# A pre-norm transformer block in fp32: from the seventh batch on, projections read the raw input transposed by the host, and the norm is applied to their products

## The chip, the cores and the metric

The kernel runs on one core of a Trainium2 chip. The metric is device time in microseconds of one execution, as a median over several runs. The profile was taken of one further execution; a clock share of 1.000 means that TensorE was never throttled in it.

TensorE multiplies matrices (PE in the profile; PEld are its weight loads), VectorE (DVE) and ScalarE (ACT) work element by element, GpSimd (POOL) does masks and small things, and SyncE (SP) issues DMA transfers. Each engine executes its own instructions in order. PSUM is the memory that TensorE writes to.

## What is computed

One layer over 16 batches of 256 tokens with 256 channels, all in fp32. Cut from the reference:

```python
def _layernorm(x, axis=-1, eps=1e-05):
    m = jnp.mean(x, axis=axis, keepdims=True)
    v = jnp.var(x, axis=axis, keepdims=True)
    return (x - m) / jnp.sqrt(v + eps)

def attn(x, wq, wk, wv, wo):                # 16 heads of 16, S = 256
    q, k, v = x @ wq.T, x @ wk.T, x @ wv.T  # split into heads
    scores = einsum('bihd,bjhd->bhij', q, k) * HEAD_DIM ** -0.5
    scores = where(j - i > 16, -inf, scores)
    return einsum('bhij,bjhd->bihd', softmax(scores), v) @ wo.T

def ffn(h, gate_w, up_w, down_w):           # 256 -> 1024 -> 256
    return (silu(h @ gate_w.T) * (h @ up_w.T)) @ down_w.T

x = x + attn(_layernorm(x), wq, wk, wv, wo)
x = x + ffn(_layernorm(x), gate_w, up_w, down_w)
```

The three feed-forward weights are not given but interpolated from control points (Catmull-Rom splines).

## The kernel before

Everything is written out in order. Five wrappers, one for each engine, keep every instruction in program order (line 88 is the wrapper, so nearly every instruction has L88 in the profile). What the profile calls `x8` for `pq` are four matmuls: an fp32 matmul leaves two records there, an fp32 transpose one.

The outer loop (line 647) runs 20 steps `s`. In step `s` three batches are in work at once: the maxima of the scores of batch `nb = s - 1`, the exponentials and value products of batch `tb = s - 2`, and the division, output projection, second norm and feed-forward of `ob = s - 3` and of the one before it. A step alternates `inner` and `outer` blocks of scores (four inner, two outer) with other work in seven gaps; `project(s, gap)` and `fill(s, gap)` say what goes into a gap. The scores of `nb` and of `tb` share two PSUM tiles. VectorE reads the maxima from them (`z`, `mx`), ScalarE the exponentials (`e`). A block of scores can only start when both have been through with the block before.

Around the change these stages matter:

- `stats_a`, `norm_a` (lines 225 to 229): mean and variance of a batch's tokens on VectorE, the power -1/2 on GpSimd (`rstda`), then `xna = (x - mean) * rstd` on VectorE, with two instructions.
- `turn_a` (231): four transposes on TensorE (`pta`) into PSUM, one copy on ScalarE into `xnT`.
- `project_qk` (235): four matmuls for q (`pq`) and four for k (`pk`) from `xnT`; ScalarE copies them to `qkc`, q times 1/4. `spread` (252): eight DMA transfers bring `qkc` to the layout of the scores (`qk`). `project_v` (262): four matmuls (`pv`), two ScalarE copies into `v`.
- `turn_max` (387): maxima transposed (`pm`), copied (`mxT`) and sent by four small transfers into `qk`, where the next step's scores of that batch subtract them.
- `gather`, `invert`, `divide`, `project_o` (417 to 467): the value products `au` are moved to `ac`, the softmax sums to `den`; their reciprocals go out to DRAM (`rd`) and come back broadcast (`rb`); `ac` is multiplied by them, projected (`py`) and added to `x`. `stats_f`, `norm_f`, `turn_f` make the second norm's `xnf`, `ptf`, `x2T`; `gate_up` (`pg`, `pu`) and `down` (`pd`) are the feed-forward.

From step 4 on `project` is regular: with `pb = s + 2`, statistics of `pb + 1` in gap 1, norm of `pb + 1` and projection and spread of `pb` in gap 2, the turn of `pb + 1` in gap 4, v of `pb` in gap 6. In steps 0 to 3 the dictionary `projections` says which stage goes where; the dictionary `heads` says in which gaps the spline weights are made (`spline`, tiles `pw`) and how many idle matmuls (`keep_running`, tile `run`) are put in.

PSUM has two buffers each for the pools `ps_f` (tag f: `pg`, `pu`, `pd`, `run`, half of `pw`) and `ps_m` (tag m: `pq`, `pk`, `pv`, `po`, `pta`, `py`, `ptf`, `pm`, the other half of `pw`). All transfers but the first few are issued by SyncE, in program order; a transfer that has to wait holds up what is issued after it. Each transfer also waits until the eighth before it has landed.

In the first microseconds ScalarE's queue loads the four attention weights; SyncE's loads `x` of batches 0 and 1, the spline table `tab`, control points `cp_in` (three parts), `x` of batch 2, the selection mask `second`, and `x` of batch 3.

Of the kernel before, what the change touches and what calls it, by code (L numbers as in the profile page):

```python
# [18 lines left out]
P = 128  # L19
# [74 lines left out]
def block_kernel(  # L94
    ctx: ExitStack,
    tc: tile.TileContext,
    x: bass.AP,
    wqT: bass.AP,
    wkT: bass.AP,
    wvT: bass.AP,  # L100
# [11 lines left out]
    const = ctx.enter_context(tc.tile_pool(name="const", bufs=1))  # L112
    sb = ctx.enter_context(tc.tile_pool(name="sb", bufs=2))
    sb1 = ctx.enter_context(tc.tile_pool(name="sb1", bufs=1))
    sb4 = ctx.enter_context(tc.tile_pool(name="sb4", bufs=4))
    sb6 = ctx.enter_context(tc.tile_pool(name="sb6", bufs=6))
    sbx = ctx.enter_context(tc.tile_pool(name="sbx", bufs=10))
# [5 lines left out]

    xs = {}

    def load_x(b, engine):
        xs[b] = sbx.tile([P, 2, DIM], F32, tag="x", name=f"x{b}")
        engine.dma_start(xs[b], x[b].rearrange("(c p) d -> p c d", p=P))

    AHEAD = 2  # L130
    load_x(0, sp)
    w_in = {}
    for nm, src in (("q", wqT), ("k", wkT), ("v", wvT), ("o", woT)):
        t = const.tile([P, 2, DIM], F32, tag=f"w{nm}", name=f"w{nm}")
        act.dma_start(t, src.rearrange("(kc p) o -> p kc o", p=P))
        w_in[nm] = t
    load_x(1, sp)
    tab_in = const.tile([P, NPART + 2 * P], F32, tag="tab", name="tab_in")
    sp.dma_start(tab_in, tab)
    cp_in = const.tile([P, 3, NPART], F32, tag="cp", name="cp_in")  # L140
    second_in = const.tile([P, 2, NROW], mybir.dt.uint8, tag="second", name="second_in")
    for w in range(3):
        sp.dma_start(cp_in[:, w, :], cps[w])
        if w == 0:
            load_x(2, sp)
            sp.dma_start(second_in, second)
    load_x(3, sp)


    ident = const.tile([P, P], F32, tag="ident", name="ident")  # L150
    make_identity(nc, ident)
    neghalf = const.tile([P, 2], F32, tag="neghalf", name="neghalf")
    pool.memset(neghalf, -0.5)
    mask0 = const.tile([P, JB], F32, tag="mask0", name="mask0")
    mask1 = const.tile([P, S], F32, tag="mask1", name="mask1")
    masks = (mask0, mask1)
# [26 lines left out]
    downT = const.tile([P, 8, DIM], F32, tag="downT", name="downT")  # L183


    xns, xnTs, mxs, aus, aos, recs, x2s, x2Ts = ({} for _ in range(8))
    es, inters, qkcs = {}, {}, {}

    moments = {}
# [1 line left out]
    def norm_stats(b, nm):  # L191
        stats = sb.tile([P, 2, 6], F32, tag=f"stats{nm}", name=f"stats{nm}{b}")
        mv = sb.tile([P, 2, 2], F32, tag=f"mv{nm}", name=f"mv{nm}{b}")
        for c in range(2):
            dve.bn_stats(stats[:, c, :], xs[b][:, c, :])
            dve.bn_aggr(mv[:, c, :], stats[:, c, :])
        rstd = sb.tile([P, 2], F32, tag=f"rstd{nm}", name=f"rstd{nm}{b}")
        dve.tensor_scalar_add(rstd, mv[:, :, 1], EPS)
        pool.tensor_tensor(rstd, rstd, neghalf, ALU.pow)
        moments[b, nm] = mv, rstd  # L200
# [24 lines left out]
    def stats_a(b):  # L225
        norm_stats(b, "a")

    def norm_a(b):
        xns[b] = normed(b, "a")

    def turn_a(b):
        xnTs[b] = sb.tile([P, 2, S], F32, tag="xnT", name=f"xnT{b}")
        transposed(xns.pop(b), xnTs[b], f"ta{b}")

    def project_qk(b):
        qkcs[b] = qkc = sb.tile([P, 2, 2, S], F32, tag="qkc", name=f"qkc{b}")
        for i, nm in enumerate("qk"):
            pq = ps_m.tile([P, 2, S], F32, tag="m", name=f"p{nm}{b}")
            for oc in range(2):
                for kc in range(2):  # L240
                    pe.matmul(
                        pq[:, oc, :],
                        lhsT=w_in[nm][:, kc, oc * P : (oc + 1) * P],
                        rhs=xnTs[b][:, kc, :],
                        start=(kc == 0),
                        stop=(kc == 1),
                    )
            act.activation(
                qkc[:, i], pq, AF.Copy, scale=HD**-0.5 if nm == "q" else 1.0
            )  # L250

    def spread(b):
        qkc = qkcs.pop(b)
# [8 lines left out]
    def project_v(b):  # L262
        pv = ps_m.tile([P, 2, DIM], F32, tag="m", name=f"pv{b}")
        for c in range(2):
            for kc in range(2):
                pe.matmul(
                    pv[:, c, :],
                    lhsT=xnTs[b][:, kc, c * P : (c + 1) * P],
                    rhs=w_in["v"][:, kc, :],
                    start=(kc == 0),  # L270
                    stop=(kc == 1),
                )
        for c in range(2):
            act.copy(
                vs[b % NQK][:, c, :, 0:HD],
                pv[:, c, :].rearrange("p (h d) -> p h d", d=HD),
            )
        del xnTs[b]

# [41 lines left out]
    def inner(nb, tb, g):  # L323
        has_n, has_t = 0 <= nb < B, 0 <= tb < B
        qn, qt = qks[nb % NQK], qks[tb % NQK]
        if has_n:
            if g == 0:
                mxs[nb] = sb.tile([P, 2, H], F32, tag="mx", name=f"mx{nb}")
            scores(qn, True, g, P, S, P + HB + LOOK)
        if has_t:  # L330
            scores(qt, False, g, HB, HB - LOOK, S - HB + LOOK)
        if has_n:
            scores(qn, True, g, P + HB, S, S)
        if has_t:
            scores(qt, False, g, 0, 0, S)
        def exponentials(pr):
            e = sb6.tile([P, 2, S], F32, tag="e0", name=f"e0{tb}_{g}_{pr}")
            act.activation(e, tiles[pr][:, :, 0:S], AF.Exp)

            pool.affine_select(  # L340
                out=e[:, :, 0:M0], in_=e[:, :, 0:M0],
                compare_op=ALU.is_ge, fill=0.0, base=LOOK,
                pattern=[[0, 2], [1, M0]], channel_multiplier=-1,
            )
            es[tb, 0, g, pr] = e

        def maxima(pr):
            for r in (2 * pr, 2 * pr + 1):
                find_max(nb, g, r, 1, S, S)

        read(exponentials if has_t else None, maxima if has_n else None)

    def outer(nb, tb, g2):
# [10 lines left out]
        def exponentials(pr):  # L364
# [4 lines left out]
                    :, :, :, W0 - W1 : W0  # L369
                ],  # L370
                AF.Exp,
            )
            pool.affine_select(
                out=e[:, :, :, 0:P], in_=e[:, :, :, 0:P],
# [181 lines left out]
    def do(stage, b, *args):  # L556
        if 0 <= b < B:
            stage(b, *args)

    heads = {
        (0, 7): (0, 6),
        (1, 1): (1, 0), (1, 4): (1, 2), (1, 5): (1, 2), (1, 6): (0, 5), (1, 7): (0, 5),
        (2, 1): (1, 0), (2, 3): (1, 6), (2, 5): (1, 1), (2, 6): (0, 4),
        (3, 3): (0, 5), (3, 6): (0, 6),
    }
    parts = iter([(w, part) for part in range(2) for w in range(2)] + [(2, 0), (2, 1)])

    def keep_running(n):
        run = ps_f.tile([P, 2 * S], F32, tag="f", name="run")
# [2 lines left out]

    def fill(s, gap):

        n, idle = heads.get((s, gap), (0, 0))
        if idle:
            keep_running(idle)  # L580
        for _ in range(n):
            spline(*next(parts))

        alone = s > B
        late = s >= B - AHEAD
        for what, at in (
# [9 lines left out]

    projections = {
        (0, 1): ((stats_a, 1),),  # L600
        (0, 2): (
            (norm_a, 1), (coefficients, 0), (coefficients, 1), (stats_a, 2),
            (scores_and_values, 1), (scores_and_values, 2), (project_qk, 0), (spread, 0),
        ),
        (0, 4): ((turn_a, 1), (norm_a, 2)),
        (0, 6): ((project_v, 0),),
        (1, 1): ((turn_a, 2), (coefficients, 2)),
        (1, 2): ((project_qk, 1), (spread, 1)),
        (1, 3): ((project_qk, 2), (spread, 2), (scores_and_values, 3)),
        (1, 6): ((project_v, 1),),  # L610
        (1, 7): ((stats_a, 3), (norm_a, 3), (project_v, 2)),
        (2, 1): ((turn_a, 3), (stats_a, 4), (scores_and_values, 4)),
        (2, 2): ((norm_a, 4), (project_qk, 3), (spread, 3)),
        (2, 4): ((turn_a, 4),),
        (2, 6): ((project_v, 3),),
        (2, 7): ((stats_a, 5), (norm_a, 5), (project_qk, 4)),
        (3, 1): ((turn_a, 5), (stats_a, 6)),
        (3, 2): ((norm_a, 6), (spread, 4), (project_qk, 5), (spread, 5)),
        (3, 3): ((project_v, 4),),
        (3, 4): ((turn_a, 6),),  # L620
        (3, 6): ((project_v, 5),),
    }

    def project(s, gap):
        if s < 4:
            todo = projections.get((s, gap), ())
        else:
            pb = s + AHEAD
            todo = {
                1: ((stats_a, pb + 1),),  # L630
                2: ((norm_a, pb + 1), (project_qk, pb), (spread, pb)),
                4: ((turn_a, pb + 1),),
                6: ((project_v, pb),),
            }.get(gap, ())
        for stage, b in todo:
            do(stage, b)


    for t in tiles:
# [7 lines left out]
    for s in range(B + 4):  # L647
# [5 lines left out]
        fill(s, 1)  # L653
        inner(nb, tb, 1)
        do(invert, ob)
        if s + 2 + AHEAD < B:
            load_x(s + 2 + AHEAD, sp)
        project(s, 2)
        fill(s, 2)
        outer(nb, tb, 0)  # L660
# [7 lines left out]
        inner(nb, tb, 3)  # L668
        do(project_o, ob)
        do(stats_f, ob)  # L670
        fill(s, 5)
        do(norm_f, ob)
        outer(nb, tb, 1)
        fill(s, 6)
        do(turn_f, ob)
        project(s, 6)
        do(turn_max, nb)
        project(s, 7)
        fill(s, 7)
# [29 lines left out]
```

## Time and profile before

| | us |
|---|---|
| median of three runs | 673.51 |
| lowest and highest of them | 672.9, 677.17 |
| the profiled execution's own time | 670.9 |
| its span, first to last instruction | 669.2 |

| engine | busy us | share of the span |
|---|---|---|
| TensorE, matmuls | 652.2 | 97% |
| VectorE | 358.5 | 54% |
| ScalarE | 230.3 | 34% |
| GpSimd | 128.1 | 19% |

The instructions concerned, from the page's groups: `pta` 64 transposes, 287 ns mean; `xnT` 16 ScalarE copies of 588 ns; `xna` 32 VectorE instructions of 453 ns; `qkc` 32 ScalarE copies of 597 ns; `v` 32 ScalarE copies of 376 ns. A mean duration is the time from an instruction's start to its end; instructions of one engine overlap, so what a row of them takes is read from their starts, or from the chain of work, which counts each moment once. SyncE's share says nothing of the engines: only the places where something waits for its transfers matter.

### The profile page before, as it was taken

Reading aid. Unit: us, or ns where it says so; the run is one execution under the profiler, and the core shown is the slowest. Engines: PE = TensorE matmul, PEld = TensorE weight load, DVE = VectorE, ACT = ScalarE, POOL = GpSimd, SP = SyncE. Lnnn points to the kernel's source line nnn. Section 1 sums busy time; section 2 is a strip of 40 time slices with the busy share of each in tenths; the row PEclk is TensorE's granted clock in tenths of the full one; section 3 lists DMA queues with packets and bytes.
Section 4 is the critical chain, followed back from the end, with each engine's and each line's share of the span. In section 5 each row is a group of like instructions: output and inputs, shape, how many; then the busy total and the mean of one; then the engine's idle time right before and its main releaser. Section 6 shows DMA issues by size and latency. Waiting matters only on the chain.

```text
span 669.2 us, 18583 instructions
## 1 busy us (share of the span) xinstructions
PE 652.2 (97%) x7484; PEld 511.6 (76%) x7484; DVE 358.5 (54%) x1473; ACT 230.3 (34%) x413; POOL 128.1 (19%) x250
## 2 busy tenths in 40 slices
PE   7999989999999999999999999999999999999998
PEld 6666767877778787777878777787877777776876
DVE  6576556556464645645464564545455565623332
ACT  2345434243342424334242433423233333333110
POOL 5222212111121211112121121211112121212000
PEclk9999999999999999999999999999999999999999
DMA  8422142113030210313031121303010101010100
GB/s 253 64 40 35 37 82 61 35 23 66 24 77 19 66 33 20 65 27 73 20 72 27 22 63 27 59 19 62 22 30 24 25 14 36 18 45 24 34 17 16
DMA packets 34422, 29.65 MB, mean 44 GB/s; under 512 B 7840, under 2 KB 33696, under 8 KB 34336
## 3 DMA queue, kind: packets, MB, share of 16 engines
q1 hardware_dynamic: 32928, 27.15, 18.1%
q10 hardware_dynamic: 1408, 1.31, 0.7%
q8 instruction: 59, 0.97, 0.6%
q14 instruction: 27, 0.22, 0.1%
HBM read 10.88 MB, written 4.46 MB: 23 GB/s over the span
## 4 chain that ended last, share of the span: by engine, by line
PE 94%; ACT 2%; DVE 2%; DMA 1%; issue 1%; POOL 0%; SPq 0%; ACTq 0%; DVEq 0%
PE pg L88 18%; PE pd L88 17%; PE pu L88 17%; PE scores L88 14%; PE po L88 6%; PE pq L88 5%; PE py L88 5%; PE pk L88 4%; PE pv L88 4%; PE pta L88 1%; PE ptf L88 1%; PE run L88 1%; PE pw L88 1%; ACT e L88 1%; DMA qk<-qkc 1%
## 5 line engine op out<-in xcount | busy, mean ns | idle before, releaser
L88 ACT ACTIVATE e<-scores 128x512 f32<-128x512 f32 (+1 forms) x192 | 117.4, 615 | 252.2 <-PE scores L88 188.5
L88 DVE CUSTOM_DVE_ANT_0 z<-scores,mask 128x144 bf16<-128x144 f32 (+1 forms) x512 | 154.4, 362 | 71.4 <-PE scores L88 36.7
L88 POOL TENSOR_SCALAR_AFFINE_SELECT e<-e 128x224 f32<-128x224 f32 (+1 forms) x192 | 94.6, 493 | 421.4 <-ACT e L88 420.9
L88 PE MATMUL pg<-x2T,gateT 128*128 128x256 f32 x512 | 125.1, 387 | 2.8 <-ACT x2T L88 2.8
L88 PE MATMUL pu<-x2T,upT 128*128 128x256 f32 x512 | 121.0, 379 | 0.0
L88 PE MATMUL pd<-downT,inter 128*128 128x256 f32 x512 | 117.0, 382 | 0.0
L88 DVE SCALAR_TENSOR_TENSOR th<-th,pg 128x512 f32<-128x512 f32 x64 | 44.0, 687 | 132.7 <-ACT th L88 132.7
L88 PEld LDWEIGHTS pg<-x2T,gateT 128*128 128x128 f32 x512 | 92.3, 190 | 21.2 <-ACT x2T L88 4.2
L88 PE MATMUL scores<-qk 17*64 17x144 f32 (+7 forms) x4096 | 105.7, 317 | 2.2 <-ACT e L88 1.1
L88 PEld LDWEIGHTS pu<-x2T,upT 128*128 128x128 f32 x512 | 97.3, 190 | 13.2
L88 PEld LDWEIGHTS pd<-downT,inter 128*128 128x128 f32 x512 | 96.1, 190 | 14.0 <-issue 0.2
L88 PEld LDWEIGHTS scores<-qk 17*64 17x64 f32 (+1 forms) x4096 | 68.6, 131 | 37.8 <-issue 29.2
L88 ACT ACTIVATE th<-pg 128x512 f32<-128x512 f32 x64 | 38.2, 597 | 69.7 <-PE pg L88 69.2
L88 DVE TENSOR_TENSOR inter<-th,pu 128x512 f32<-128x512 f32 x64 | 44.0, 688 | 26.1 <-PE pu L88 26.1
L88 PE MATMUL po<-e,v 128*32 128x256 f32 (+1 forms) x1024 | 50.0, 335 | 0.1
L88 PEld LDWEIGHTS po<-e,v 128*32 128x32 f32 x1024 | 29.6, 109 | 23.3 <-issue 12.5
L88 DVE DVE_READ_ACCUMULATOR2_ANT mx<- 128x1 f32 x512 | 42.2, 82 | 0.0
L88 DVE TENSOR_TENSOR x<-x,pd 128x256 f32<-128x256 f32 x32 | 13.5, 421 | 51.9 <-PE pd L88 51.9
L88 PE MATMUL pq<-xnT,wq 128*128 128x256 f32 x128 | 31.9, 392 | 1.2 <-ACT xnT L88 0.7
L88 PE MATMUL py<-wo,ac 128*128 128x256 f32 x128 | 31.8, 391 | 1.1 <-ACT e L88 1.1
L88 PE MATMUL pv<-wv,xnT 128*128 128x256 f32 x128 | 30.6, 382 | 0.8 <-ACT v L88 0.6
L88 PEld LDWEIGHTS py<-wo,ac 128*128 128x128 f32 x128 | 23.1, 189 | 9.5 <-issue 4.6
(54 smaller groups left out, 414.7 us busy)
## 6 DMA issues: line engine op xcount, KB each, us to landing
qk<-qkc SPq DMA_DIRECT2D x124, 64.0 KB
x<-x SPq DMA_DIRECT2D x16, 256.0 KB
ac<-au SPq DMA_DIRECT2D x128, 32.0 KB
rb<-rd SPq DMA_DIRECT2D x32, 128.0 KB
out<-x SPq DMA_DIRECT2D x15, 256.0 KB
qk<-mxT SPq DMA_DIRECT2D x64, 4.0 KB
den<-au SPq DMA_DIRECT2D x64, 4.0 KB
cp_in<-cps SPq DMA_DIRECT2D x3, 256.0 KB
```

The source lines that it names most:

```text
L88: return self.tc.keep_in_program_order(fn(*args, **kwargs))
```

## The change

The host passes a second copy of the input, `xT`, with channels before tokens. Batches 0 to 5 go as before (`RAW = 6`). For batches 6 to 15 `norm_a` and `turn_a` are gone: `xT` is loaded by DMA and q, k and v are projected from it. The mean is taken out by the weights: TensorE multiplies `wq`, `wk` and `wv` by a matrix of 1/256 (`sum_weights`), and VectorE subtracts the result from them in place (`center`), in step 3, after batch 5's projection of each. The factor `rstd` is applied to the products. For v it differs by partition, and ScalarE's copy takes it as its scale. For q and k it differs along the free dimension: `send_factors` writes the 256 factors to DRAM, `spread_factors` reads them back to all partitions (`fa`), and VectorE multiplies `pq` and `pk` by it on the way to `qkc`, in place of ScalarE's copy. The 1/4 on q moves into the exponential's scale for all batches.

The loads of the head are in another order: `wo` moves to the end of SyncE's list, and `second`, the second and third part of `cp_in`, and `x` of batches 3 and 4 are issued after batch 0's spread instead of before it. `heads` and `projections` are merged into one dictionary, `early`. With it, in step 1 gap 7 four of five idle matmuls stand before `project_v` of batch 2 rather than after it; in step 2 gap 1 a spline part stands before `stats_a`; in step 3 the idle matmuls are gone, and `project_v` of batch 5 comes before `turn_f`.

```diff
-    load_x(0, sp)
+    load_x(0)
...
-    for nm, src in (("q", wqT), ("k", wkT), ("v", wvT), ("o", woT)):
...
-    load_x(1, sp)
+    for nm, src in (("q", wqT), ("k", wkT), ("v", wvT)):
+        load_weight(nm, src, act)
+    load_x(1)
...
+    sp.dma_start(cp_in[:, 0, :], cps[0])
+    load_x(2)
+
+    def load_rest(_):
+
+        sp.dma_start(second_in, second)
+        sp.dma_start(cp_in[:, 1, :], cps[1])
+        load_x(3)
+        sp.dma_start(cp_in[:, 2, :], cps[2])
+        load_x(4)
+        load_weight("o", woT, sp)
...
+    def sum_weights(nm):
+        sums[nm] = ps_f.tile([P, DIM], F32, tag="f", name=f"sum{nm}")
+        for kc in range(2):
+            pe.matmul(
+                sums[nm], lhsT=means, rhs=w_in[nm][:, kc, :], start=(kc == 0), stop=(kc == 1)
+            )
+
+    def center(nm):
+        for kc in range(2):
+            dve.tensor_tensor(
+                w_in[nm][:, kc, :], w_in[nm][:, kc, :], sums[nm], ALU.subtract
+            )
+
+    factors, across = {}, {}
+
+    def send_factors(b):
+        _, factors[b] = moments.pop((b, "a"))
+        across[b] = dr.tile([S], F32, tag="ra", name=f"ra{b}")
+        sp.dma_start(across[b].rearrange("(c p) -> p c", p=P), factors[b])
+
+    def spread_factors(b):
+        to = sb3.tile([P, S], F32, tag="fa", name=f"fa{b}")
+        sp.dma_start(to, across[b].unsqueeze(0).to_broadcast([P, S]))
+        across[b] = to
...
-            act.activation(
-                qkc[:, i], pq, AF.Copy, scale=HD**-0.5 if nm == "q" else 1.0
-            )
+            if b < RAW:
+                act.copy(qkc[:, i], pq)
+            else:
+                dve.tensor_tensor(
+                    qkc[:, i], pq, across[b].unsqueeze(1).to_broadcast([P, 2, S]), ALU.mult
+                )
...
-            act.copy(
+            act.activation(
                 vs[b % NQK][:, c, :, 0:HD],
                 pv[:, c, :].rearrange("p (h d) -> p h d", d=HD),
-            )
-        del xnTs[b]
+                AF.Copy,
+                scale=1.0 if b < RAW else factors[b][:, c : c + 1],
+            )
+        del xTs[b]
...
-            act.activation(e, tiles[pr][:, :, 0:S], AF.Exp)
+            act.activation(e, tiles[pr][:, :, 0:S], AF.Exp, scale=HD**-0.5)
...
+        (1, 7): (
+            (stats_a, 3), (norm_a, 3), (keep_running, 4), (project_v, 2), (keep_running, 1),
+        ),
+        (2, 1): ((turn_a, 3), (part, 3), (stats_a, 4), (scores_and_values, 4)),
...
-        (3, 2): ((norm_a, 6), (spread, 4), (project_qk, 5), (spread, 5)),
-        (3, 3): ((project_v, 4),),
-        (3, 4): ((turn_a, 6),),
-        (3, 6): ((project_v, 5),),
+        (3, 2): ((spread, 4), (project_qk, 5), (spread, 5), (send_factors, 6)),
+        (3, 3): ((project_v, 4), (sum_weights, "q"), (sum_weights, "k")),
+        (3, 4): ((center, "q"), (center, "k"), (spread_factors, 6)),
+        (3, 6): ((project_v, 5), (sum_weights, "v"), (center, "v")),
...
+        pb = s + AHEAD
+        for stage, b, at in (
+            (stats_a, pb + 1, 1),
+            (project_qk, pb, 2),
+            (spread, pb, 2),
+            (send_factors, pb + 1, 2),
+            (spread_factors, pb + 1, 4),
+            (project_v, pb, 6),
+        ):
+            if at == gap:
+                do(stage, b)
...
-        if s + 2 + AHEAD < B:
-            load_x(s + 2 + AHEAD, sp)
+        if s:
+            do(load_x, s + 2 + AHEAD)
+            if s + 1 + AHEAD >= RAW:
+                do(load_xT, s + 1 + AHEAD)
...
+        if s == 3:
+            project(s, 6)
         do(turn_f, ob)
-        project(s, 6)
+        if s != 3:
+            project(s, 6)
```

## The prediction

> **What bounds the kernel now.** I read the page first, then busy time by stretch, then the chain of waits inside one step, then the timelines of VectorE and of SyncE's queue at the places that the change touches. All times are microseconds of the profiled execution: span 669.2, its own time 670.9 (1.7 outside the span). The median of the runs shown is 673.51, 2.6 above; I carry my difference over to it.
>
> The page's first part, and busy time by stretch (columns: us, PE, PEld, DVE, ACT, POOL, PEclk, DMA share, GB/s):
>
> ```profile
> PE 652.2 (97%) x7484; PEld 511.6 (76%) x7484; DVE 358.5 (54%) x1473; ACT 230.3 (34%) x413; POOL 128.1 (19%) x250
> ```
>
> ```profile
> 0.00:17.40 17.40, 13.30 (x72) 11.24 (x72) 11.20 (x25) 4.20 (x7) 9.06 (x22) 1.00 0.82 248
> 17.40:43.00 25.60, 24.67 (x254) 16.88 (x262) 15.78 (x78) 7.73 (x16) 3.38 (x6) 1.00 0.37 54
> 43.00:95.00 52.00, 48.17 (x771) 34.77 (x756) 32.62 (x165) 26.75 (x49) 15.89 (x31) 1.00 0.28 52
> 95.00:517.00 422.00, 421.72 (x5009) 334.28 (x5008) 233.02 (x987) 150.91 (x271) 79.63 (x153) 1.00 0.18 41
> ```
>
> From 95 to 517 (steps 4 to 13, one of 38.87 each while batches are still projected) TensorE lacks 0.28 us of 422: there only TensorE's work counts. Before 95 it lacks 8.9 us, and waits matter. After 517 nothing that the diff touches runs.
>
> The chain within step 8, with batch 11's turn in it, and within step 13, where no batch is left to turn:
>
> ```profile
> 270.69 1.49 PE po L88 x32
> 272.18 0.59 PE pta L88 x4
> 272.77 1.73 PE pg L88 x8
> ```
>
> ```profile
> 465.06 1.49 PE po L88 x32
> 466.55 1.92 PE pg L88 x8
> ```
>
> This is the change's main term, already in the trace: without pta, pg follows po directly and takes 1.92 instead of 1.73. So four transposes are worth 0.59 - 0.19 = 0.40, not 0.59. The distance between the py of neighbouring steps agrees: 432.69 - 393.81 = 38.88 with a turn, 471.17 - 432.69 = 38.48 without.
>
> VectorE in step 8, where the q and k products will be made (duration in the second column, idle time before in brackets):
>
> ```profile
> 262.89 0.54 DVE L88 RECIPROCAL rec<-den 64x64 f32<-64x64 f32 x1
> 263.35 0.65 DVE L88 TENSOR_SCALAR xna<-x,mva,rstda 128x256 f32<-128x256 f32 x2
> 266.27 0.31 DVE L88 CUSTOM_DVE_ANT_0 z<-scores,mask 128x144 bf16<-128x144 f32 x1 [2.26 <-ACT qkc L88]
> ```
>
> SyncE's queue in step 3, and VectorE and TensorE in the same step:
>
> ```profile
> 82.49 12.02 SPq L88 DMA_DIRECT2D qk<-qkc  x16
> 96.03 2.30 SPq L88 DMA_DIRECT2D qk<-mxT  x4
> ```
>
> ```profile
> 86.02 0.69 DVE L88 TENSOR_TENSOR ac<-ac,rb 128x512 f32<-128x512 f32 x1 [1.65 <-DMA qk<-qkc]
> ```
>
> ```profile
> 86.81 1.97 PE L88 MATMUL py<-wo,ac 128*128 128x256 f32 x8 [1.12 <-ACT e L88]
> ...
> 92.57 0.78 PE L88 MATMUL ptf<-ident,xnf 128*128 128x128 f32 x4 [1.19 <-DVE xnf L88]
> 93.19 1.89 PE L88 MATMUL pv<-wv,xnT 128*128 128x256 f32 x8
> ```
>
> Here TensorE waits on a chain, ac, py, x, statistics, xnf, ptf; and SyncE issues without a pause up to 94.5, then the four small mxT transfers that step 4's scores need.
>
> **What the Trainium skill says.** "TensorE: Matmul & The Clock Gate", Part 4 (PE-mode transpose), gives about 275 ns for a 128x128 transpose inside a kernel. The record's median here is 273, but four in a row take 0.44 (ptf) to 0.59: they overlap, and the chain's price decides. "VectorE: DVE Perf Modes", the perf-mode tier table, leaves a tensor_tensor with fp32 or a PSUM operand in the slowest mode, 1x; x<-x,py, the same shape as the new products, takes 687 ns, and I use that. "DMA: Bandwidth & Descriptors", Anatomy of one DMA (of a transfer that GpSimd issues), gives some 2 us fixed, mostly the receipt of the write; here, from SyncE, batch 0's last spread issue ends at 15.82 and the wait for it at 17.44, 1.62 us later.
>
> **The change, part by part.**
>
> *Turns, steps 4 to 12 (batches 7 to 15).* Nine times 0.40: -3.6, by the step distances 9 x 0.39 = -3.5. I take -3.5; the low end is 9 x 0.59 = -5.3, should pg's surcharge not return. ScalarE loses xnT (0.59) and both qkc copies (2 x 0.60), but is 34% busy: worth nothing.
>
> *Products on VectorE.* Two of 0.69 replace xna (0.65 for two). Q's starts when the reciprocal ends, 263.4; k's needs pk, which ends at 264.99, so it ends near 265.7. The maxima queued behind begin at 266.27 now: 0.55 left. Later maxima would hold the second exponential, and TensorE only at the next inner scores (269.72), which need the tiles; the maxima end at 268.2, so some 1.5 more is spare. Cost nothing; if the cover went, each microsecond past 2.0 would cost ten. V's factor on ScalarE costs nothing likewise (376 ns each, engine idle around it).
>
> *Loads in the steps.* xT (256 KB, one issue of 0.45) stands after the reciprocals' broadcast rb and before the spread; it is read a step later, and the spread two steps later. The factors go out (ra, 256 pieces of 4 bytes) after the spread and come back (fa) for the next step. fa waits on SyncE for ra's landing, but out and mxT come over 10 us later (issues in step 5: spread ends 158.0, out 171.2). Nothing.
>
> *Step 3, the changeover.* Its own pta (0.59) lies in front of the wait for ac: worth nothing. Sums of q and k (4 matmuls, 1.73 as for pk) replace five idle ones (1.11): the inner scores and their maxima come 0.6 later, end 85.0. Four centring instructions follow, at most 0.42 each by x<-x,pd, some 1.5: the division starts at 86.4, not 86.0: +0.4 on py, x and xnf. Then pv and the sum of v (1.73 + 0.87) fill the wait before ptf, where six idle matmuls (1.3) stood, and pv no longer lies behind ptf. That would give back 1.7, but pm needs maxima that follow xnf (94.5 now, so 95.0), and x2T, which pg needs, now stands on ScalarE behind the v copies (0.65). I get pg at 95.9 against 95.31: +0.6. Without these two waits it would be -0.6.
>
> On SyncE, mxT is now behind one xT (0.45), ra (about 0.5), the wait for ra's landing (1.6, plus up to 0.95 for 16 small packets per DMA engine at the 59 ns that a packet takes on average: 18.1% of 16 x 669.2 over 32,928) and fa (0.65). From 94.5 that gives 97.7 to 98.7 instead of 96.03, so the first mxT is issued (0.58) by 98.3 to 99.3 and lands 1.6 later, at 99.9 to 100.9. Scores of the old batch need it at 98.77 + 0.24 = 99.0 before, 99.6 with the later pg. A new wait of 0.3 to 1.3, once; I take 0.9. Step 3 together: +1.5, bounds -0.6 and +3.
>
> *Head.* The first spread has 1.5 MB less in front of it (second, two cp_in, x3, x4, wo are moved behind it or off ScalarE's queue). Yet its end is set by four issues (2.96) and 1.62: I take -0.3 (bounds 0 and -1.2). cp_in's second part is then issued near 16.7, should land by 19.5, and VectorE asks for it at 20.0: no wait. In step 1's last gap four idle matmuls (0.89) move in front of pv of batch 2, which waits 0.57 for ScalarE: it starts at 39.76, not 39.43, but one idle matmul (0.22) stands behind it instead of five (1.11): -0.8 (bounds 0 and -0.9). Head: -1.1.
>
> Sum: -3.5 - 1.1 + 1.5 = -3.1. The span becomes 666.1, the execution's own time 667.8, the median 673.5 - 3.1 = 670.4.
>
> **Rivals.**
>
> *A, the forecast:* the steps give 0.40 each, head and changeover nearly cancel: 670.4, own range 667.5 to 673.
>
> *B, clearly faster:* the changeover's reordering pays and the fa wait hides. Steps -3.5 to -5.3, head -2.1, step 3 -0.6: -6.2 to -8.0, or 665.5 to 667.3. For it: pv does leave the place behind ptf, and 4.1 us of TensorE's gaps lie before 17.4. Against it: the two waits named, and step 13's 1.92.
>
> *C, slower:* ra's round trip at step 3. SyncE's queue has no slack there, and mxT, so step 4's scores, wait behind it; every microsecond over 1.6 for 256 four-byte writes is paid once. It outweighs the gain when the round trip exceeds some 5 us, and passes 1% (6.7) near 12: about 681. For it: the trace has no transfer of 4-byte pieces. Against it: 59 ns a packet, and den's 256-byte pieces cause no wait. The same price on every step would need 15 us, since later steps have that slack.
>
> *D, the change doesn't do what it says:* the removed transposes were cover. Excluded by step 13, which runs without them and without a gap.
>
> **How the numbers follow.** A 0.69, B 0.25, C 0.06. A measurement of this kernel can tell about 1% from no change, 6.7 us: A is within it, B about at or beyond it, C beyond on the other side. Hence faster 0.25, same 0.69, slower 0.06. The range reaches from B's end with the runs' scatter (663.5) to A with the changeover at its worst (675), and leaves C out.
>
> **What would show it.** Right: a step of 38.48 between the py of steps 4 to 12; pg directly after po at 1.92; VectorE's maxima in the second gap still starting right after their scores; mxT at step 3 issued more than a microsecond later than xT alone explains, with a short wait of the scores on it; first scores still near 17. Wrong: any gap of TensorE in the steady steps, pg of step 3 earlier than 95.3 relative to the first scores, a wait of cp_in in step 1, or a step shorter than 38.4.

## The result, and the profile after

| | median us | lowest to highest | ratio to the kernel before, 95% interval |
|---|---|---|---|
| before, beside it | 674.74 | 669.9 to 678.11 | |
| after | 678.12 | 675.8 to 685.34 | 1.0059 [1.0036, 1.0082] |

The changed kernel is slower by 0.6%, 3.4 us. The forecast of 670.4 and its range of 663.5 to 675 are both missed, on the side of rival C. The profiled execution of after took 679.66 (span 677.9), 8.7 more in span than that of before, which lies near the low end of its kernel's runs.

The page's first part, and busy time by stretch, of after (columns as before: us, PE, PEld, DVE, ACT, POOL, PEclk, DMA share, GB/s):

```profile
PE 655.8 (97%) x7434; PEld 511.8 (75%) x7434; DVE 368.5 (54%) x1479; ACT 215.0 (32%) x383; POOL 128.1 (19%) x251
```

```profile
0.00:17.40 17.40, 13.99 (x63) 12.03 (x64) 10.52 (x24) 3.04 (x4) 10.25 (x25) 0.90 0.44 139
...
95.00:517.00 422.00, 414.80 (x4870) 326.08 (x4871) 236.99 (x975) 136.06 (x241) 77.89 (x149) 0.99 0.23 50
```

TensorE has fewer instructions and yet is busy longer. In the first stretch its clock is 0.90, and in the long stretch it lacks 7.2 us, where before lacked 0.28. The chain of waits says where. First the changeover from step 3 to step 4, then later steps of after (start, us, engine, tile):

```profile
96.55 7.16 DMA ra<-rstda
104.15 4.03 DMA qk<-mxT
```

```profile
127.68 1.49 PE po L88 x32
129.17 1.92 PE pg L88 x8
133.79 1.92 PE py L88 x8
...
172.28 1.92 PE py L88 x8
```

In the later step pg follows po directly at 1.92, and the py of neighbouring steps are 38.49 apart: that is the gain as forecast. At the changeover a DMA stands on the chain: the trip of the factors to DRAM, 7.16, then the maxima behind it. SyncE's queue and TensorE's timeline of after, at that place:

```profile
84.78 11.67 SPq L88 DMA_DIRECT2D qk<-qkc  x16
96.55 0.53 SPq L88 DMA_DIRECT2D ra<-rstda  x1
103.72 0.34 SPq L88 DMA_DIRECT2D fa<-ra  x1
104.15 2.31 SPq L88 DMA_DIRECT2D qk<-mxT  x4
```

```profile
96.53 0.39 PE L88 MATMUL pm<-ident,mx 128*16 128x128 f32 x2 [1.66 <-ACT v L88]
97.01 3.36 PE L88 MATMUL pg<-x2T,gateT 128*128 128x256 f32 x8
...
108.23 1.82 PE L88 MATMUL scores<-qk 17*64 17x208 f32 x24 [5.30 <-DMA qk<-mxT]
109.98 2.90 PE L88 MATMUL po<-e,v 128*32 128x256 f32 x32
112.81 2.84 PE L88 MATMUL pg<-x2T,gateT 128*128 128x256 f32 x8
```

Read it in this order. The issue of ra ends at 97.08. SyncE then stands until 103.72, 6.64 us, because fa may not be issued before ra has landed. So mxT goes out at 104.15, where before issued it at 96.03, and TensorE stands 5.30 for it. The second loss is in the durations: pg and po take 3.36 and 2.90, where the same work at full speed takes 1.9 and 1.56. The granted clock (the column behind POOL) shows it too:

```profile
90.00:100.00 10.00, 8.25 (x92) 6.15 (x91) 5.47 (x26) 2.69 (x6) 2.01 (x4) 0.87 0.49 72
100.00:110.00 10.00, 4.70 (x44) 2.78 (x44) 1.37 (x2) 0.60 (x1) 0.00 (x0) 0.84 0.16 17
110.00:120.00 10.00, 10.00 (x92) 7.10 (x89) 5.53 (x24) 3.57 (x6) 1.83 (x4) 0.77 0.07 14
```

What is missing from 1.00 in these three stretches comes to 5.2 us of clock.

Between py of step 3 and py of step 4 after takes 45.45 (88.34 to 133.79), before 34.89 (86.81 to 121.70). By the starts on TensorE's timeline the 10.56 between them are, to within rounding: the wait, 5.30; matmuls at about half speed, 1.4 and 0.4 (pg and pu of step 3), 1.4 (scores, with their restart), 1.3 (po) and 0.8 (pg of step 4), together 5.3; the way to pg of step 3, 0.3; step 4's transposes gone, -0.4.

### The profile page after: what moved, and what is told of

It is laid out like the page before. It is cut to its first block, busy times and chain, and to the rows that moved or that the text cites. A ratio compares the mean times of both kernels' runs of the same rounds, so it can differ in the third digit from the quotient of the medians.

```text
span 677.9 us, 18514 instructions
## 1 busy us (share of the span) xinstructions
PE 655.8 (97%) x7434; PEld 511.8 (75%) x7434; DVE 368.5 (54%) x1479; ACT 215.0 (32%) x383; POOL 128.1 (19%) x251
## 4 chain that ended last, share of the span: by engine, by line
PE 90%; DMA 3%; DVE 2%; ACT 2%; issue 1%; POOL 1%; SPq 0%; ACTq 0%; DVEq 0%
PE pg L88 18%; PE pd L88 17%; PE pu L88 16%; PE scores L88 14%; PE po L88 6%; PE py L88 5%; PE pq L88 4%; PE pk L88 4%; PE pv L88 3%; DMA ra<-rstda 1%; DMA x<-x 1%; PE ptf L88 1%; PE pw L88 1%; ACT e L88 1%; PE run L88 1%
## 5 line engine op out<-in xcount | busy, mean ns | idle before, releaser
L88 PE MATMUL pg<-x2T,gateT 128*128 128x256 f32 x512 | 128.3, 394 | 2.9 <-ACT x2T L88 2.8
L88 PE MATMUL scores<-qk 17*64 17x144 f32 (+7 forms) x4096 | 107.2, 318 | 7.9 <-DMA qk<-mxT 5.3
L88 PEld LDWEIGHTS pg<-x2T,gateT 128*128 128x128 f32 x512 | 93.7, 192 | 24.4 <-DVE mx L88 4.7
L88 PE MATMUL pq<-xT,wq 128*128 128x256 f32 x128 | 33.5, 407 | 1.2 <-ACT xT L88 0.7
L88 PEld LDWEIGHTS pq<-xT,wq 128*128 128x128 f32 x128 | 24.1, 198 | 9.8 <-issue 4.4
L88 PE MATMUL pv<-wv,xT 128*128 128x256 f32 x128 | 30.6, 382 | 0.2 <-ACT qkc L88 0.2
```

The source lines that it names most:

```text
L88: return self.tc.keep_in_program_order(fn(*args, **kwargs))
```

## The experiments

Each kernel is after with the edit shown, and is compared with runs of the kernel before on the same chip (medians of before 672.5 to 673.74). "Trip" is the time from the end of ra's issue to the issue of fa where nothing else stands between them on the queue; it includes all that holds fa back.

### Take the maxima out from behind the trip

```diff
-        (3, 4): ((center, "q"), (center, "k"), (spread_factors, 6)),
+        (3, 4): ((center, "q"), (center, "k")),
...
+        (3, 7): ((spread_factors, 6),),
```

> The changed kernel with one move: at step 3 the factors of batch 6 come back (fa) after the four mxT transfers, in gap 7, instead of in gap 4 before them. Theory W (SyncE waits 6.6 us at fa for ra's landing, mxT is late, TensorE stands 5.3 us and then works slowly for some microseconds): mxT at step 3 is issued within 0.3 us of its copy, no wait of scores on mxT, pg, pu, scores and po of steps 3 and 4 at their usual length; 7 to 10 us less than the changed kernel, ratio to the kernel before about 0.993 to 0.997. Theory H (the loss lies in the head's load order): no more than 1 us less than the changed kernel, ratio 1.003 to 1.008.

Measured: 672.24, ratio 0.9982 [0.996, 1.0004]; that is 5.9 less than after, where 7 to 10 were expected. fa alone moves, behind mxT. SyncE's queue and TensorE of this kernel:

```profile
96.68 0.53 SPq L88 DMA_DIRECT2D ra<-rstda  x1
97.83 2.30 SPq L88 DMA_DIRECT2D qk<-mxT  x4
103.61 0.34 SPq L88 DMA_DIRECT2D fa<-ra  x1
```

```profile
97.02 0.39 PE L88 MATMUL pm<-ident,mx 128*16 128x128 f32 x2 [1.65 <-ACT v L88]
97.50 3.29 PE L88 MATMUL pg<-x2T,gateT 128*128 128x256 f32 x8
```

mxT goes out 6.3 earlier, the scores wait only 0.4 for it, and the loss against before is gone, though no gain is shown (the interval holds 1). So fa's place in SyncE's queue causes the loss. Two things are left over. pm still stands 1.65, and pg behind it is slow. And mxT takes long: in this kernel's chain it stands for 5.60 from its first issue, where it took 4.03 in after.

```profile
97.83 5.60 DMA qk<-mxT
```

### The order of the loads

Here the loads go back to the old order: `second`, `cp_in`, x3, x4 in SyncE's queue at the start, wo in ScalarE's.

```diff
-    for nm, src in (("q", wqT), ("k", wkT), ("v", wvT)):
+    for nm, src in (("q", wqT), ("k", wkT), ("v", wvT), ("o", woT)):
...
-        (0, 2): (
-            (norm_a, 1), (project_qk, 0), (spread, 0), (load_rest, 0), (coefficients, 0),
+        (0, 2): (
+            (norm_a, 1), (project_qk, 0), (spread, 0), (coefficients, 0),
```

> The changed kernel with the head's loads in the order of the kernel before (wo on ScalarE's queue, second, cp_in and x of batches 3 and 4 before batch 0's spread). Theory H: first scores near 17.5 instead of 19.5, pq of batch 0 at its usual 1.99 instead of 3.62, and about 2 us less than the changed kernel. Theory W: the wait of the scores on mxT at step 3 stays near 5 us and the ratio to the kernel before stays above 1.002; if the late first scores were chance and not the load order, nothing changes.

Measured: 678.45, ratio 1.0069 [1.0042, 1.0096]; after has 1.0059. The scores at step 3 wait 6.43 for mxT here. The loads' order does neither good nor harm that these runs can tell.

### Idle matmuls in the wait

```diff
+        (3, 7): ((keep_running, 24),),
```

> The changed kernel with 24 idle matmuls (about 5.3 us) at the end of step 3, behind turn_max, where TensorE is about to wait for mxT; the wait on SyncE is left as it is. If the loss there is the wait alone, the time stays the same within 1 us or grows. If the slow matmuls behind the wait (po 2.83 instead of 1.49, pg 2.77 instead of 1.92, scores 1.82) come from TensorE's standing still, they are back at their usual length, and the time falls by 2 to 4 us against the changed kernel although the wait for mxT remains.

Measured: 677.71, ratio 1.006 [1.0036, 1.0084]. TensorE of this kernel:

```profile
98.26 5.52 PE L88 MATMUL run<-ident 128*128 128x128 f32 x48
103.62 1.89 PE L88 MATMUL pg<-x2T,gateT 128*128 128x256 f32 x8
...
110.55 1.52 PE L88 MATMUL scores<-qk 17*64 17x208 f32 x24 [2.80 <-DMA qk<-mxT]
```

In this profile pg ran at full speed, 2.80 of the wait stayed, and po behind it was slow again (2.69). The clocks of all runs say more: their mean is 0.994 here (15 runs) and 0.990 in after (22 runs), some 2.7 us of clock bought back. So less half speed comes where less of the wait is left empty. The median hardly moves, since the filler stands in front of pg and costs about as much.

### Idle matmuls at the start

The edit of the first experiment, and 18 instead of 12 idle matmuls at the start of the kernel.

```diff
-    keep_running(12)
+    keep_running(18)
```

> As the kernel with fa behind mxT, and the run of idle matmuls at the very start longer: 18 instead of 12, so that TensorE is busy until about 7.3, when the first transposes come. If pq of batch 0 is slow (3.62 instead of 1.99) because TensorE stood still before it, pq is back near 2 us and the median is 1 to 2 us below the kernel with fa moved alone. If the first transposes get delayed instead, it is 0 to 1 us above.

Measured: 672.61, ratio 0.9981 [0.9961, 1.0], as without them. pq of batch 0 now ran at full speed (1.99 instead of 3.34), but py (3.49) and pg (3.51) of step 3 at half: the slow stretch had moved.

### Take away pm's wait

pm can't have its PSUM buffer before ScalarE has copied v out of it. With the first experiment's edit, pv and v's centring go behind `turn_f`, and only v's sum stays in front:

```diff
-        (3, 6): ((project_v, 5), (sum_weights, "v"), (center, "v")),
+        (3, 6): ((project_v, 5), (center, "v")),
...
         if s == 3:
-            project(s, 6)
+            sum_weights("v")
         do(turn_f, ob)
-        if s != 3:
-            project(s, 6)
+        project(s, 6)
```

> fa behind mxT, and at step 3 project_v and the centring of v behind turn_f as in every other step; only the sum of v stays in front of it. With project_v in front, pm stood 1.65 us for the v copies and pg ran at half clock behind it. If that order costs, pm's wait goes, pv covers x2T's copy, pg of step 3 is at its usual length more often, and the median is 1 to 3 us below the kernel with fa moved alone (672.2), ratio to the kernel before 0.994 to 0.997. If pv in front of ptf was the gain it was written for, the time rises by 1 to 2 us, since TensorE then stands in front of ptf.

Measured: 671.59, ratio 0.9974 [0.9956, 0.9993]; whether it is quicker than the first experiment's kernel isn't shown, since the intervals overlap. pm's wait is gone and pg took 1.89, but the scores of this kernel waited:

```profile
102.78 1.82 PE L88 MATMUL scores<-qk 17*64 17x208 f32 x24 [2.11 <-DMA qk<-mxT]
```

mxT was issued at 97.42, 1.2 after ra's issue ended, and the scores had it over 5 us later. So ra seems to delay what is transferred behind it too, and not only fa; in the first experiment pm's wait and the slow pg and pu had hidden most of that. The kernel with 512 pieces, below, confirms it.

### Send the factors earlier

Against after, only ra moves, ahead of the spreads of step 3:

```diff
-        (3, 2): ((spread, 4), (project_qk, 5), (spread, 5), (send_factors, 6)),
+        (3, 2): ((send_factors, 6), (spread, 4), (project_qk, 5), (spread, 5)),
```

> The changed kernel with ra of batch 6 issued in front of the two spreads of step 3 rather than behind them; fa stays where it is, in front of mxT. Theory W (the wait of fa on ra's landing, not the two issues themselves): the wait goes, since 16 spread issues (11.7 us) now lie between ra and fa; mxT is issued about 1 us later than without the two, and the time is that of the kernel with fa moved, 672 plus or minus 1. If the issues themselves or the transfers' data held mxT, it stays near 678.

Measured: 671.19, ratio 0.9956 [0.9937, 0.9976]. SyncE's queue of this kernel:

```profile
84.97 0.40 SPq L88 DMA_DIRECT2D ra<-rstda  x1
85.81 14.19 SPq L88 DMA_DIRECT2D qk<-qkc  x16
100.04 0.58 SPq L88 DMA_DIRECT2D fa<-ra  x1
100.72 2.29 SPq L88 DMA_DIRECT2D qk<-mxT  x4
```

The trip now runs beside the spreads, and mxT follows fa at once. Not all of it is hidden: the spreads' issues take 14.19 instead of 11.67. This one moved word turns the change from slower to faster.

### Other numbers and sizes of pieces

With fa moved as in the first experiment, ra goes out as 128 pieces of 8 bytes, as 512 of 4 bytes (every factor twice), or as 128 of 64 bytes. The edit of the first of them:

```diff
-        sp.dma_start(across[b].rearrange("(c p) -> p c", p=P), factors[b])
+        sp.dma_start(across[b].rearrange("(p c) -> p c", p=P), factors[b])
```

> The price of ra's round trip by itself, read from the trace of the kernel with fa behind mxT at steps 4 and later (end of ra's issue to fa's issue, 6.6 us with 256 pieces of 4 bytes). Here ra is 128 pieces of 8 bytes; the two halves of the factors then come back in another order, so q and k get wrong factors. If the trip grows with the pieces, it is 3.5 to 4.5 us; if it is fixed, it stays at 6.6. The time of the kernel stays within 2 us of 672.

> As before, with 512 pieces of 4 bytes: the factors are written twice, after two small GpSimd copies, and the first half is read back. If the trip grows with the pieces, it is 11 to 13 us from the end of ra's issue to fa's issue at steps 4 and later; if it is fixed, it stays at 6.6. fa is still read a step later, so the time stays within 2 us of 672.

> ra as 128 pieces of 64 bytes (each factor 16 times, after a GpSimd copy), of which fa reads the first 1 KB back, so q and k get wrong factors. 128 pieces of 8 bytes took 3.3 us from the end of ra's issue to fa's issue, 256 of 4 bytes 6.6, 512 of 4 bytes 7.3, so neither the number of pieces nor the bytes alone set it. If neighbouring pieces that fall close together in DRAM hold each other up (64 of 8 bytes and 128 of 4 bytes lie in 512 bytes), the trip falls to 2.0 to 2.6 us although eight times the bytes are written. If each piece has its price wherever it lies, it stays near 3.3.

The first and the third of these kernels leave out what would bring each token's own factor back, so q and k of batches 6 to 15 are wrong in them; they serve to time the trip alone.

Measured, one time each: 667.14, 677.19 and 667.11; the first two are some 5 from the 672 that was expected. The trips, read at step 4 of the kernels with 512 pieces and with 64-byte pieces:

```profile
130.26 0.54 SPq L88 DMA_DIRECT2D ra<-two  x1
138.29 0.34 SPq L88 DMA_DIRECT2D fa<-ra  x1
```

```profile
120.61 0.54 SPq L88 DMA_DIRECT2D ra<-many  x1
122.50 0.34 SPq L88 DMA_DIRECT2D fa<-ra  x1
```

From the end of ra's issue to fa: 7.49 and 1.35. With 8-byte pieces it was 3.32, in after 6.57 at the same step. So the trip isn't a fixed time: 8 times the bytes in half as many pieces take a fifth of it. Nor does it go by the number of pieces alone, since 512 take little longer than 256, where 11 to 13 had been expected.

At step 3 of the kernel with 512 pieces the maxima stand right behind ra:

```profile
97.59 2.30 SPq L88 DMA_DIRECT2D qk<-mxT  x4
```

```profile
106.31 1.82 PE L88 MATMUL scores<-qk 17*64 17x208 f32 x24 [3.43 <-DMA qk<-mxT]
```

From their first issue to the scores that need them it is 8.72 here and 5.36 with 256 pieces (v behind `turn_f`), while with the two short trips no scores waited for them. So what is transferred behind ra on this queue is delayed by it, the more so the longer ra's trip.

The two short trips ran at clock 1.000 throughout, with a span of 665.4 each against 669.2 and 668.8 of before at clock 1.000. So without half speed on either side the change is worth 3.4 to 3.8, where the maxima don't wait.

> The kernel before, profiled once more. Its first profile had full clock throughout and took 670.9, while its median is 673.6. If the half clock strikes it too, by where TensorE's waits fall, this execution, when it is slower than 672, shows one to three stretches of about 3.4 us of slow matmuls in steps 0 to 3, each worth 1.5 to 2 us, and otherwise the same instruction times. If its scatter has another source, the clock is 1.000 and the extra time lies elsewhere.

That second profile of before: 670.52, span 668.8. It wasn't one of the slower executions, so it doesn't say what they lose; the clocks of all runs do, further down.

### The doses, with nothing moved

This answers the main question alone. Everything stands as in after; only the trip is shorter. First the 64-byte pieces, with a small GpSimd copy in front. As above this kernel doesn't restore the right factors, so its time is a measurement and not a version to use:

```diff
-        across[b] = dr.tile([S], F32, tag="ra", name=f"ra{b}")
-        sp.dma_start(across[b].rearrange("(c p) -> p c", p=P), factors[b])
+        across[b] = dr.tile([P * 16], F32, tag="ra", name=f"ra{b}")
+        many = sb4.tile([P, 16], F32, tag="many", name=f"many{b}")
+        pool.tensor_copy(many, factors[b][:, 0:1].to_broadcast([P, 16]))
+        sp.dma_start(across[b].rearrange("(p c) -> p c", p=P), many)
...
-        sp.dma_start(to, across[b].unsqueeze(0).to_broadcast([P, S]))
+        sp.dma_start(to, across[b][0:S].unsqueeze(0).to_broadcast([P, S]))
```

> The changed kernel with nothing moved; only ra is 128 pieces of 64 bytes, whose trip took 1.35 us, of which fa reads the first 1 KB, so q and k get wrong factors. If the length of ra's trip is the term that was mis-sized, the wait of the scores on mxT at step 3 falls from 5.3 us to under 1, and the time to 668.5 to 671.5, ratio to the kernel before 0.993 to 0.998: the forecast's -3. If the order of the queue or the rest of step 3 carries the loss, it stays above 675.

Then 8-byte pieces, in DRAM in the order that `factors` has, with the products reading `fa` in steps of two (they still take 0.64 and 0.69), which gives the right factors:

```diff
-        sp.dma_start(across[b].rearrange("(c p) -> p c", p=P), factors[b])
+        sp.dma_start(across[b].rearrange("(p c) -> p c", p=P), factors[b])
...
+                by = across[b].rearrange("q (p c) -> q c p", c=2)
                 dve.tensor_tensor(
-                    qkc[:, i], pq, across[b].unsqueeze(1).to_broadcast([P, 2, S]), ALU.mult
+                    qkc[:, i].rearrange("q o (c p) -> q o c p", c=2),
+                    pq.rearrange("q o (c p) -> q o c p", c=2),
+                    by.unsqueeze(1).to_broadcast([P, 2, 2, P]),
+                    ALU.mult,
                 )
```

> The changed kernel with nothing moved; ra is 128 pieces of 8 bytes (the two factors of a partition side by side), and the products read fa with a step of two, so that the factors are right again. With a trip of 3.3 us instead of 6.6 the wait of the scores on mxT is 1.5 to 2.5 us instead of 5.3. The time follows the trip: 671 to 675, between the changed kernel (678) and the one with the short trip. If the products with a step of two are slower than 0.69, VectorE's row shows it, and up to 2 us each cost nothing.

SyncE's queue of the first, then SyncE's queue and TensorE of the second:

```profile
96.04 0.53 SPq L88 DMA_DIRECT2D ra<-many  x1
98.38 0.34 SPq L88 DMA_DIRECT2D fa<-ra  x1
98.81 2.30 SPq L88 DMA_DIRECT2D qk<-mxT  x4
```

```profile
96.88 0.53 SPq L88 DMA_DIRECT2D ra<-rstda  x1
100.88 0.34 SPq L88 DMA_DIRECT2D fa<-ra  x1
101.31 2.30 SPq L88 DMA_DIRECT2D qk<-mxT  x4
```

```profile
104.58 1.42 PE L88 MATMUL scores<-qk 17*64 17x208 f32 x24 [3.38 <-DMA qk<-mxT]
```

| kernel | trip at step 3 | wait for mxT | median | ratio to before |
|---|---|---|---|---|
| 64-byte pieces | 1.81 | none | 670.84 | 0.9966 [0.9948, 0.9985] |
| 8-byte pieces | 3.47 | 3.38 | 673.61 | 0.9993 [0.9971, 1.0016] |
| after, 4-byte pieces | 6.64 | 5.30 | 678.12 | 1.0059 [1.0036, 1.0082] |

With a trip as long as the prediction assumed, the prediction's time comes out: 670.8 against 670.4, or 2.9 less than before against 3.1. Each microsecond of trip then costs 1.1 to 1.4 (0.0027 of 674 for 1.66, 0.0066 of 674 for 3.17), and the gain is used up at a trip of about 3.8. The interval of the middle row leaves about a microsecond to either side open. The wait with 8-byte pieces was longer than the 1.5 to 2.5 expected.

### A better version

Three edits together: ra ahead of the spreads, fa behind the maxima, pv behind `turn_f`. The second kernel also has idle matmuls (six in step 3, 18 at the start); the third has the first's order with the 8-byte pieces.

> Three moves at step 3: ra in front of the spreads, fa behind mxT, project_v and the centring of v behind turn_f. With fa alone behind mxT, ra's slow pieces still lie in front of mxT on the same queue, and the scores still waited 2.1 us for mxT in one profile. If those pieces are what is left, mxT lands within 2 us of its issue, there is no wait of the scores on it, and the median is 1 to 2 us below the kernel with fa and v moved (671.6): about 670, ratio to the kernel before 0.993 to 0.996. If what is left is TensorE's half clock by chance, it stays at 671 to 672.

> As the kernel with the three moves at step 3, and TensorE kept busy where it stood: six idle matmuls behind the sum of v in front of turn_f at step 3, and 18 instead of 12 at the start. If standing still for 1 to 2 us brings the half clock, it comes less often: mean clock 0.997 or more, median 669 to 670.5, ratio 0.991 to 0.995. If it comes whatever TensorE does there, the median is that of the kernel with the three moves, within 0.5 us.

> The pieces of 8 bytes and the three moves at step 3 together (ra in front of the spreads, fa behind mxT, v behind turn_f). The trip lies wholly beside the spreads in both cases, so it should equal the kernel with the three moves within 1 us: 669 to 671, ratio 0.993 to 0.998. If the slow pieces also hold up the spreads' data on the queue, it is up to 1 us less.

Measured: 669.8, ratio 0.9956 [0.9936, 0.9976]; with idle matmuls 671.37, 0.9983 [0.9961, 1.0004]; with 8-byte pieces 668.77, 0.9937 [0.9919, 0.9954]. The idle matmuls were a miss. The mean clock of the runs is 0.996 with and without them, so they bought nothing there, and in the profile those at the start push back batch 0's first transposes (8.24 against 7.34 without them); in the earlier kernel with 18 they hadn't (7.26). SyncE's queue of the best kernel:

```profile
84.62 0.40 SPq L88 DMA_DIRECT2D ra<-rstda  x1
85.47 11.53 SPq L88 DMA_DIRECT2D qk<-qkc  x16
100.26 2.28 SPq L88 DMA_DIRECT2D qk<-mxT  x4
102.58 0.44 SPq L88 DMA_DIRECT2D fa<-ra  x1
```

There nothing waits for mxT. This version beats both kernels: before by 0.6%, after by 1.2% (1.0059 / 0.9937). Moving ra alone has nearly all of it (0.9956). Whether the 8-byte pieces add to the order isn't shown, since the intervals overlap. The trace has a reason why they might: the issues of the spreads behind ra take 11.53 with them, and 14.07 with 4-byte pieces in the same order.

## Why the prediction was wrong

**Steps 4 to 12, forecast -3.5: right.** The py are 38.49 apart (forecast 38.48), pg follows po at 1.92, and TensorE has no new gap in the steady steps of after.

**Products on VectorE, forecast nothing: right.** They take the durations forecast, and the maxima behind them still start at once after their scores. VectorE of after, step 8:

```profile
274.27 0.65 DVE L88 TENSOR_TENSOR qkc<-pq,fa 128x512 f32<-128x512 f32 x1
275.95 0.69 DVE L88 TENSOR_TENSOR qkc<-pk,fa 128x512 f32<-128x512 f32 x1 [1.03 <-PE pk L88]
277.18 0.31 DVE L88 CUSTOM_DVE_ANT_0 z<-scores,mask 128x144 bf16<-128x144 f32 x1 [0.54 <-PE scores L88]
```

The idle 0.54 before the maxima, ended by the scores, is the cover that the prediction counted as 0.55.

**Head.** The -0.8 in step 1 was right: from batch 0's first scores to pq of batch 3 after takes 0.85 less (first scores 2.02 later than before, pq 1.17 later). The -0.3 for the loads did not come: in a kernel with the new order and batch 0's pq at full speed (64-byte pieces, fa moved) the first scores start 0.15 later than before. After's profile has them 2.02 later: 1.63 because pq of batch 0 took 3.62 instead of 1.99, and 0.40 because the first transposes started later (7.28 against 6.88).

**Step 3, forecast +1.5, bounds -0.6 and +3: here it failed.** The term is "the wait for ra's landing (1.6, plus up to 0.95 for 16 small packets per DMA engine at the 59 ns that a packet takes on average". It measured 6.64. Both parts came from rows that bear no likeness to ra: the 1.6 from a spread of 64 KB, and the 59 ns from a mean over packets of some 825 bytes (27.15 MB in 32,928). The path was right: fa waits for ra, mxT stands behind fa, and the scores wait for mxT. That wait was forecast at 0.9 and measured 5.30. Step 3 together came to some +6 without half speed (0.7 up to pg, 5.3 of wait) and some +11 with it. The trace of before has no transfer of 4-byte pieces, as the text itself said under rival C, and the upper bound should have come from that ignorance, not from the mean. The way up to pg was sized well, in part by luck: pg of step 3 starts 1.86 later than before and pq of batch 3 1.17, so 0.69 is lost between (forecast +0.6), but pm waits 1.66 there for the PSUM buffer that ScalarE's v copies hold, which no step named.

**A term that wasn't there: half speed.** TensorE stood 1.66 for pm and 5.30 for mxT, and parts of the work behind ran at about half speed, some 5.3 in this profile. The prediction had nothing for it. How much of the time it is can be read from the mean clock of each run. First the kernel before, by the 190 that were taken beside the experiments (two more, of 946.0 and 1302.12, are left out). The four commonest values:

| mean clock of the run | runs | their mean time |
|---|---|---|
| 1.000 | 24 | 670.7 |
| 0.997 | 66 | 672.5 |
| 0.995 | 35 | 674.8 |
| 0.992 | 30 | 676.5 |

So the scatter of before goes with the clock (correlation -0.92 over the 190), and a step of 0.0025 is 3.3 us at half speed (0.0025 x 669 x 2). The mean of all is 0.996; after has 0.990, and no run above 0.995. An estimate from these: taking (1 - clock) x span off each run, the median of after is 672.5 and that of before 670.2 to 671.0 on the four chips. Some 1.5 to 2.3 are thus lost to the wait less the gain, and half speed takes some 3.6 more than in before. (The before runs in the table of the result have no clock on record; their median, 674.74, is higher than the 672.5 to 673.74 of these.) The profiles' terms agree with the first: -3.5 for the steps, -0.8 for step 1, +0.7 up to pg and +5.3 for the wait are +1.7.

The Trainium skill, "TensorE: Matmul & The Clock Gate", Part 1, gives a reason for half speed: a clock gate that halves the clock after an idle window of 3413 ns, with windows that run on regardless of the work. The trace agrees on the size: pq of batch 0 lost 1.63, which is 3.3 us at half speed. It doesn't fully agree on the cause, since here waits under 2 us were followed by it in some executions (pg of step 3 at 3.36 in after, 1.99 with the same wait in the kernel with 8-byte pieces in place). So in this kernel a microsecond of waiting can cost more than a microsecond, with chance in it.

**The short trip's 670.8** is close to the forecast partly because terms cancel: the wait of 0.9 and the head's -0.3 did not come, and half speed took some 0.8 more than in before (mean clock 0.9945 against 0.9957).

**Rival C** had the mechanism and the place, SyncE's queue without slack in step 3. Its break-even of "some 5 us" was high, if anything: some 3.8 by the doses, with about a microsecond open to either side. The chance of 0.06 rested on the same 59 ns and on den's 256-byte pieces, and these are no evidence for 4-byte ones. That later steps have slack held as far as it was tried: the trip took 6.57 at step 4 as well, and nothing waited there; 15 us was never reached.

**What stays open.** Why 256 pieces of 4 bytes take so long. The Trainium skill, "DMA: Bandwidth & Descriptors", Specifications, says that transfers under 512 bytes are done by read-modify-write. The runs agree that small pieces are slow, but 64-byte pieces, also under 512, took 1.35 to 1.81 and no longer than the wait for a spread. Pieces that lie close together, 128 to a stretch of 512 bytes, may hold each other up, or pieces under 64 bytes may be slow each by itself. That 512 pieces took only 0.9 longer than 256 speaks against pieces that are slow one after another, but no run here settles it. What length of wait brings half speed stays open too.

## What to carry to other kernels

Where a change sends data out and waits for it to come back, look at what stands behind the wait on the same queue, and move the sending ahead or the wait behind before anything is measured; here one word's place was worth 1%. What is sent behind slow small pieces on the same queue is late too, even where it doesn't wait for them. A transfer whose shape the trace doesn't have gets no price from the mean of other transfers: take its bound from what would hurt, and let the chance follow from that. A wait of TensorE in a kernel that is 97% busy is to be reckoned dearer than its length. Where runs scatter, set their mean clock beside their times before looking for another reason.

## What the runs showed of the hardware

- A trip of 1 KB from SBUF to DRAM, until the next transfer that reads it can be issued: 6.6 us as 256 pieces of 4 bytes (6.64 and 6.57 in after), 3.2 to 3.5 as 128 of 8 bytes; 2 KB as 512 of 4 bytes 7.5; 8 KB as 128 of 64 bytes 1.35 to 1.8.
- Four small transfers issued behind such a trip on the same queue, while it was under way, were there for the scores 5.4 to 5.6 us after their first issue (256 pieces) and 8.7 (512 pieces), against 4.0 where the trip had ended.
- With 256 pieces of 4 bytes in front of them, 16 spreads took 14.1 to 15.3 us to issue; with 128 of 8 bytes 11.5, and 11.5 to 12.3 with none.
- After TensorE stood for 1 to 2 us, stretches at half speed followed in some executions and not in others. The mean clock of the runs went down in steps of about 0.0025, each worth some 1.7 to 2.3 us.
